# One attention kernel, three edits to its transfers: values stored in reading order, a head's large loads on ScalarE's queue, queries fetched four rows at a time

## The chip, the core and the metric

The kernel runs on one core of one Trainium2 chip. The metric is the device time of one execution in microseconds (us). Before the change, six runs gave a median of 5294.02 us (5281.08 to 5301.66).

## What is computed

The input is an image batch of 4 x 384 channels x 32 x 32. Two layers follow. Layer 0 is attention with relative positions, then a small feed-forward block. Layer 1 is a 7 x 7 depthwise convolution (several kernels folded into one), then a mixture of four experts. All of it is float32. Only the attention of layer 0 and the projections ahead of it are touched here:

```python
qkv = (xt @ w_qkv).reshape(b, n, 3, HEADS, hd).transpose(2, 0, 3, 1, 4)   # b=4, n=1024, 8 heads, hd=48
q, k, v = qkv[0] * scale, qkv[1], qkv[2]
attn = einsum('bhid,bhjd->bhij', q, k)
attn = attn + take_along_axis(einsum('bhid,hLd->bhiL', q, table_k), idx)          # 15 x 15 clipped offsets
attn = attn + take_along_axis(einsum('bhjd,hLd->bhjL', k * scale, table_q), idx).T
attn = softmax(attn)
out = einsum('bhij,bhjd->bhid', attn, v)
out = out + einsum('bhiL,hLd->bhid', wsum(attn, idx), table_v)
```

## The kernel before

There are three phases one after the other. The memory of one phase is given to the next, so the first instructions of a phase wait for the last transfers that read the memory of the one before.

**Projection (`qkv_phase`, 0 to 314 us).** Eight tiles of 512 tokens. Each is normalised over the channels and multiplied by the weights. Queries and keys go to a DRAM tensor `qk_d` (768 rows, one for each channel, 4096 tokens each). Values go to `v_d`, token by token: row = token, 384 channels, so that a head's part of a row is 192 bytes. The evacuations from PSUM alternate between ScalarE and VectorE. The stores are issued by GpSimd, one for `v_d` in each tile (768 KB).

**Attention (`attention_phase`, 314 to 2176 us).** The heads run one after the other. A head begins with `load_head`: the two offset tables into `tab`, the keys and the queries of all four images into `kq` (partitions 0 to 47 and 64 to 111), half of the keys again into `k2`. `prepare` multiplies tables with keys and queries: one result is transposed into `b2` in SBUF, the other goes through ScalarE copies (`st`, L218) to a DRAM scratch `sd`. Then `load_values` brings the head's values into `vb`, four DMAs of 192-byte runs; each value row is padded to 64 columns, and the padding is set to zero once.

The inner loop runs over the 32 rows `y` of the image. One step handles row `y` of all four images together (4 x 32 queries on 128 partitions). Its parts, with the lines that the profile names:

- `fetch(y + 2)`: one small DMA brings the queries of the row (`qs`, 24 KB), one brings its part of `sd` (`s1`, 240 KB, shown as `s`); GpSimd then adds the bias for the row (L249). `s1` has three buffers, so a fetch waits for an older row's bias.
- `scores`: PE multiplies queries with keys (`sc_ps`); VectorE adds the bias and takes the maximum in one instruction (L275).
- `exponentials`: ScalarE (L285).
- `far_sums` on VectorE (L296, L297), `transposes` on PE with copies by ScalarE (L305, L306), `windows` on PE and VectorE (L315, L320).
- after every four rows `values`: PE multiplies the weights with `vb` (`av_ps`), ScalarE copies the result (L338).
- after rows 15 and 31 `value_table`: the part of `table_v`, from the tile `tvw` (`tv_ps`, L367).

The tile `tvw` is loaded anew for each head in nine pieces, one in each of the rows 4 to 12: six of 384 KB with an outermost size of 4, then three of 192 KB. `normalise` (rows 2 and 18) loads the reciprocal sums into one buffer `rb`, half by half, and GpSimd multiplies (L379); `store` follows at rows 4 and 20. What is left of a head after its last row is done while the next head begins.

Order: every DMA of this phase is issued by SyncE, in the order in which the program calls `dma` (L146); PE, VectorE and ScalarE instructions are held in program order too (`pin`). SyncE can run ahead of the engines as far as its own waits allow, and an instruction that waits holds up all that is behind it on the same engine.

**Rest (`rest_phase`, 2176 to 5279 us).** Projection of the output, feed-forward, convolution and experts, one image after the other. The change doesn't touch it.

Of the kernel before, what the change touches and what calls it, by code (L numbers as in the profile page):

```python
# [10 lines left out]
F32 = mybir.dt.float32  # L11
# [6 lines left out]
P = 128  # L18
B, C, IMG = 4, 384, 32
N = IMG * IMG  # L20
NT = B * N
KC = C // P
HEADS, HD = 8, C // 8
# [4 lines left out]
NBLK = N // P  # L28
PADR = 6
AROWS = IMG + 2 * PADR  # L30
YB = 4
YT = 16
XT = 16
BIG = 3.0e38
FF = 1536
NF = FF // P
NEXP = 4
TOK = 512
# [38 lines left out]
def qkv_phase(tc, cst, x, w_qkv, qk_d, v_d):  # L77


    nc = tc.nc  # L80
    with ExitStack() as es:
        wp = es.enter_context(tc.tile_pool(name="q_w", bufs=1))
        work = es.enter_context(tc.tile_pool(name="q_work", bufs=2))
        ev = es.enter_context(tc.tile_pool(name="q_ev", bufs=4))
        psum = es.enter_context(tc.tile_pool(name="q_ps", bufs=2, space=PSUM))
        psmm = es.enter_context(tc.tile_pool(name="q_mm", bufs=4, space=PSUM))
        wq = wp.tile([P, KC, 3 * C], F32, name="wq")
        nc.sync.dma_start(wq, w_qkv.rearrange("(k p) n -> p k n", p=P))
        for t in range(NT // TOK):
            b, n0 = divmod(t * TOK, N)  # L90
            xt = work.tile([P, KC, TOK], F32, tag="xt", name="xt", bufs=3)
            nc.sync.dma_start(xt, x[b, :, n0 : n0 + TOK].rearrange("(k p) n -> p k n", p=P))
            xn = work.tile([P, KC, TOK], F32, tag="xn", name="xn")
            layer_norm(nc, (work, work, psum, "st"), cst["ones"], xt, xn, cst["eps6"])
            for m in range(2 * KC):
                ps = psmm.tile([P, TOK], F32, tag="mm", name="qk_ps")
                for k in range(KC):
                    nc.tensor.matmul(  # L98
                        ps, wq[:, k, m * P : (m + 1) * P], xn[:, k, :], start=(k == 0), stop=(k == KC - 1)
                    )  # L100
                sb = ev.tile([P, TOK], F32, tag="qk", name="qk_sb")
                if m % 2:
                    nc.vector.tensor_copy(sb, ps)
                else:
                    nc.scalar.copy(sb, ps)
                nc.gpsimd.dma_start(qk_d[m * P : (m + 1) * P, t * TOK : (t + 1) * TOK], sb)
            vs = ev.tile([P, TOK // P, C], F32, tag="v", name="v_sb", bufs=2)
            for j in range(TOK // P):
                ps = psmm.tile([P, TOK], F32, tag="mm", name="v_ps")
                for k in range(KC):  # L110
                    nc.tensor.matmul(
                        ps[:, :C], xn[:, k, j * P : (j + 1) * P], wq[:, k, 2 * C :], start=(k == 0), stop=(k == KC - 1)
                    )
                if j % 2:
                    nc.vector.tensor_copy(vs[:, j, :], ps[:, :C])
                else:
                    nc.scalar.copy(vs[:, j, :], ps[:, :C])
            nc.gpsimd.dma_start(v_d[t * TOK : (t + 1) * TOK, :].rearrange("(j p) c -> p j c", p=P), vs)


def attention_phase(tc, cst, tabs, tv, qk_d, v_d, ao_d, heads):
# [15 lines left out]
    nc = tc.nc  # L137

    def pin(ins):
        return tc.keep_in_program_order(ins)  # L140
# [3 lines left out]

    def dma(*args, **kw):
        pin(nc.sync.dma_start(*args, **kw))  # L146

    with ExitStack() as es:
        dram = es.enter_context(tc.tile_pool(name="a_dram", bufs=2, space=DRAM))
# [24 lines left out]
        kq = fixed.tile([64 + HD, NT], F32, name="kq")  # L174
        k2 = fixed.tile([64 + HD, B, N // 2], F32, name="k2")
        tab = fixed.tile([64 + HD, SPAN, ZW], F32, name="tab")
        vb = fixed.tile([P, B, NBLK, 64], F32, name="vb")
        nc.gpsimd.memset(vb, 0.0)
        b2 = fixed.tile([P, IMG, SPAN, IMG], F32, name="b2")
        b2f = b2.rearrange("p x e y -> p (x e y)")  # L180
        aT = fixed.tile([P, NBLK, YB, P], F32, name="aT")
# [4 lines left out]
            return bass.AP(ap.tensor, ap.offset + off, [list(ap.ap[0])] + dims)  # L186

        def load_head(h):
            dma(tab[0:HD], tabs[1, h])
            dma(tab[64 : 64 + HD], tabs[0, h])  # L190
            kd = qk_d[C + h * HD : C + (h + 1) * HD, :]
            dma(kq[0:HD, :], kd)
            dma(kq[64 : 64 + HD, :], qk_d[h * HD : (h + 1) * HD, :])
            dma(k2[64 : 64 + HD], kd.rearrange("p (b n) -> p b n", b=B)[:, :, N // 2 :])

        def load_values(h):
            for b in range(B):
                dma(
                    vb[:, b, :, :HD],
                    v_d[b * N : (b + 1) * N, h * HD : (h + 1) * HD].rearrange("(c p) d -> p c d", p=P),  # L200
                )

        def prepare(h):

# [19 lines left out]
                )  # L224
            return sd

        def fetch(s):

            h, y = s["h"], s["y"]
            s["qs"] = small.tile([HD, B, IMG], F32, tag="qs", name="qs")  # L230
            dma(
                s["qs"],
                qk_d[h * HD : (h + 1) * HD, :].rearrange("p (b n) -> p b n", b=B)[:, :, y * IMG : (y + 1) * IMG],
            )
            s1 = work.tile([P, SPAN, IMG], F32, tag="s1", name="s1", bufs=3)
            sd = s["sd"]
            dma(
                s1.rearrange("p e x -> p (e x)"),
                bass.AP(
                    sd.tensor, sd.offset + y * IMG * SPAN * IMG,  # L240
                    [[IMG * IMG * SPAN * IMG, B], [SPAN * IMG, IMG], [1, SPAN * IMG]],
                ),
            )
            bias = work.tile([P, IMG, IMG], F32, tag="bias", name="bias", bufs=3)
            c0, c1 = max(0, y - 6), min(IMG, y + 7)
            for y0, y1, e, step in ((c0, c1, c0 - y + 7, 1), (0, c0, 0, 0), (c1, IMG, SPAN - 1, 0)):
                if y0 < y1:
                    n = y1 - y0
                    nc.gpsimd.tensor_tensor(  # L249
                        bias[:, y0:y1, :],  # L250
                        shifted(b2f, e * IMG + y0, [[step * IMG + 1, n], [SPAN * IMG, IMG]]),
                        s1[:, e : e + n, :] if step else bcast(s1[:, e : e + 1, :], 1, n),
                        ALU.add,
                    )
            s["bias"] = bias
# [135 lines left out]
        def load_value_table(h):  # L391

            base = tv.offset + h * SPAN * ZW * HD
            for c in range(3):
                for i in range(0, IMG, IMG // 2):
                    dma(
                        tvw[:, c, i : i + IMG // 2].rearrange("p i d -> p (i d)"),
                        bass.AP(
                            tv.tensor, base + ((1 + 4 * c) * ZW + i) * HD,
                            [[ZW * HD, 4], [HD, IMG], [1, IMG // 2 * HD]],  # L400
                        ),
                    )
                    yield
            for i, e in enumerate((SPAN - 2, 0, SPAN - 1)):
                dma(
                    tvw[i * IMG : (i + 1) * IMG, 3].rearrange("p i d -> p (i d)"),
                    bass.AP(tv.tensor, base + e * ZW * HD, [[HD, IMG], [1, IMG * HD]]),
                )
                yield

        late = None
        for h in heads:
            load_head(h)
            sd = prepare(h)
            done = None
            if late is not None:
# [9 lines left out]
            for y in range(IMG):  # L426
                s = blk[y]
                if y + 2 < IMG:
                    fetch(blk[y + 2])
                if y >= 4:  # L430
                    next(pieces, None)
                if done and y % YT == 2:
                    normalise(done[1], done[2])
                if done and y % YT == 4:
                    store(done[0], done[1], done[3])
                    done = None
                if y + 1 < IMG:
                    scores(blk[y + 1])
                far_sums(s)
                bound = y % YB == 0  # L440
                if bound and y + 1 < IMG:
                    exponentials(blk[y + 1])
                if bound and y:
                    windows(blk[y - 1])
                    values(o, y - 1)
                    if y % YT == 0:
                        done = (h, o, value_table(h, o, y - 1), y - 1)
                if y % YT == 0:
                    o = work.tile([P, B // 2, YT * IMG], F32, tag="o", name="oT")
                transposes(s)  # L450
                if not bound:
                    windows(blk[y - 1])
                    if y + 1 < IMG:
                        exponentials(blk[y + 1])
# [254 lines left out]
def metaformer_kernel(ctx: ExitStack, tc: tile.TileContext, ins, out):  # L709
# [10 lines left out]
        nc.vector.memset(t, v)  # L720
        cst[name] = t
    qk_d = dram.tile([2 * C, NT], F32, name="qk_d")
    v_d = dram.tile([NT, C], F32, name="v_d")
    ao_d = dram.tile([C, NT], F32, name="ao_d")
    qkv_phase(tc, cst, ins["x"], ins["w_qkv"], qk_d, v_d)
    attention_phase(tc, cst, ins["tabs"], ins["tv"], qk_d, v_d, ao_d, list(range(HEADS)))
# [64 lines left out]
```

## Time and profile before

| | |
|---|---|
| median of six runs | 5294.02 us (5281.08 to 5301.66) |
| profiled execution | 5281.08 us, span of its instructions 5279.2 us |
| PE, VectorE, ScalarE, GpSimd busy | 82%, 46%, 23%, 19% of the span |
| granted TensorE clock, mean | 0.89 |
| phases | 0 to 314, 314 to 2176, 2176 to 5279 us |
| DMA engines busy in the three phases | 24%, 36%, 17% |
| PE busy in attention | 1422 of 1862 us |

The chain that ended last is followed back from the end of the program: at each step to what released the instruction. An entry "DMA s<-sd" there is the time from the issue of that transfer to its landing. In lists of instructions the numbers in front are the start and the duration in us; the brackets give the idle time of the engine just before, and what ended it; "SPq" is SyncE's issue of a DMA. "L285" is line 285 of the kernel.

### The profile page before, as it was taken

How to read it: one execution, taken by the hardware profiler on the slowest of the kernel's cores; microseconds unless marked ns; L12 is line 12 of the kernel's file. 1: busy time of each engine (PE TensorE's matmuls, PEld its weight loads, DVE VectorE, ACT ScalarE, POOL GpSimd, SP SyncE). 2: the span in 40 equal slices, each digit the busy share in tenths (PEclk: the TensorE clock that was granted, in tenths of full speed). 3: DMA queues.
4: the chain of work that ended last, by engine and by line, in shares of the span. 5: the costliest groups of instructions: out<-in, count | busy, mean ns of one | idle time of the engine just before them, and what ended most of it. 6: DMA issues, size and time to landing. Idle time of an engine off the chain costs nothing.

```text
span 5279.2 us, 55887 instructions
## 1 busy us (share of the span) xinstructions
PE 4349.0 (82%) x22816; PEld 2231.4 (42%) x22816; DVE 2444.9 (46%) x3220; ACT 1237.5 (23%) x2011; POOL 992.4 (19%) x798
## 2 busy tenths in 40 slices
PE   7867777877878777660789998799998899999999
PEld 3335555545555555320234343243442343444443
DVE  2237575766657576349288111494112781111111
ACT  1124443434434343210111111111112111111111
POOL 1226344353543535100000000100000000000000
PEclk9989898988889898875789899799998898989999
DMA  2242433424343342300012122022121121212211
GB/s 103 74 133 78 141 88 116 124 85 129 81 136 105 93 123 87 99 24 0 12 36 72 60 72 72 12 72 78 54 72 36 31 77 60 72 60 72 78 60 36
DMA packets 256880, 397.31 MB, mean 75 GB/s; under 512 B 100520, under 2 KB 182732, under 8 KB 255856
## 3 DMA queue, kind: packets, MB, share of 16 engines
q1 hardware_dynamic: 249584, 368.57, 23.0%
q0 software_dynamic: 7040, 25.17, 1.2%
q8 instruction: 180, 2.95, 0.2%
q14 instruction: 76, 0.62, 0.0%
HBM read 299.05 MB, written 94.63 MB: 75 GB/s over the span
## 4 chain that ended last, share of the span: by engine, by line
PE 65%; DVE 14%; DMA 8%; issue 7%; POOL 3%; ACT 3%; SPq 1%; POOLq 0%; DVEq 0%; ACTq 0%
PE y_ps L684 17%; PE e_ps L675 16%; DVE xb L642 5%; PE av_ps L143 4%; PE tabq_ps L143 3%; PE qk_ps L98 3%; DVE extra L297 3%; DMA s<-sd 2%; DMA qs<-qk_d 2%; PE sc_ps L143 2%; PE tv_ps L143 2%; PE t_ps L305 2%; PE ln_var L60 2%; DVE ln_rstd L64 2%; DMA kq<-qk_d 2%
## 5 line engine op out<-in xcount | busy, mean ns | idle before, releaser
L684 PE MATMUL y_ps<-hs,wb 128*128 128x512 f32 x2304 | 1080.4, 608 | 1.5 <-DVE hs L681 1.5
L675 PE MATMUL e_ps<-xn_e,wa 128*128 128x512 f32 x2304 | 1060.0, 600 | 0.0
L249 POOL TENSOR_TENSOR bias<-b,s 128x416 f32<-128x416 f32 (+24 forms) x656 | 791.3, 1241 | 919.3 <-DMA s<-sd 449.0
L681 DVE TENSOR_TENSOR hs<-hs,ge 128x512 f32<-128x512 f32 x384 | 263.9, 689 | 1310.7 <-ACT hs L680 1301.1
L642 DVE SCALAR_TENSOR_TENSOR xb<-img,w,xb 128x1024 f32<-128x1024 f32 x588 | 723.8, 1291 | 8.8 <-POOL img L67 8.8
L675 PEld LDWEIGHTS e_ps<-xn_e,wa 128*128 128x128 f32 x2304 | 443.4, 193 | 555.6 <-issue 555.5
L684 PEld LDWEIGHTS y_ps<-hs,wb 128*128 128x128 f32 x2304 | 417.4, 192 | 616.7 <-issue 402.6
L680 ACT ACTIVATE hs<-e_ps,c_b 128x512 f32<-128x512 f32 x384 | 263.8, 687 | 1733.7 <-PE e_ps L675 1694.6
L275 DVE CUSTOM_DVE_ANT_0 arow<-sc_ps,bias 128x1024 f32<-128x1024 f32 x256 | 311.7, 1218 | 372.2 <-POOL bias L249 277.1
L285 ACT ACTIVATE arow<-arow,nm 128x1024 f32<-128x1024 f32 x256 | 295.0, 1152 | 550.8 <-DVE nm L275 549.6
L689 POOL DMA_DIRECT2D out<-ot x8 | 6.5, 808 | 2177.5 <-DVE ot L688 2177.5
L305 PE MATMUL t_ps<-ident,arow 128*128 128x128 f32 x2048 | 311.0, 300 | 125.6 <-ACT arow L285 108.3
L143 PE MATMUL sc_ps<-kq,qs 48*32 48x512 f32 x2048 | 315.7, 682 | 102.8 <-DMA qs<-qk_d 102.8
L305 PEld LDWEIGHTS t_ps<-ident,arow 128*128 128x128 f32 x2048 | 245.1, 152 | 328.4 <-ACT arow L285 240.2
L296 DVE TENSOR_REDUCE extra<-arow 128x32 f32<-128x32 f32 (+24 forms) x512 | 354.4, 734 | 0.0
L306 ACT COPY aT<-t_ps 128x512 f32<-128x512 f32 x512 | 277.9, 588 | 294.5 <-PE t_ps L305 293.8
L60 PE MATMUL ln_var<-ln_sq,ones 128*128 128x512 f32 x192 | 127.6, 817 | 249.8 <-ACT ln_sq L57 249.8
L143 PE MATMUL sc_ps<-k,kq 48*32 48x512 f32 x2048 | 315.7, 682 | 0.0
L143 PE MATMUL av_ps<-aT,vb 128*64 128x128 f32 x4096 | 279.4, 303 | 0.0
L143 PEld LDWEIGHTS av_ps<-aT,vb 128*64 128x64 f32 x4096 | 263.9, 156 | 12.0 <-issue 7.6
L143 PE MATMUL tabq_ps<-tab,kq 48*128 48x480 f32 x512 | 229.6, 607 | 22.0 <-DMA kq<-qk_d 21.2
L143 PE MATMUL tabk_ps<-tab,kq 48*128 48x480 f32 x512 | 235.0, 615 | 15.2 <-DMA kq<-qk_d 15.2
(112 smaller groups left out, 3722.5 us busy)
## 6 DMA issues: line engine op xcount, KB each, us to landing
wa<-in_w SPq DMA_DIRECT2D x64, 1152.0 KB
wb<-in_w SPq DMA_DIRECT2D x64, 1152.0 KB
sd<-st SPq DMA_DIRECT2D x128, 480.0 KB
s<-sd SPq DMA_DIRECT2D x256, 240.0 KB
tvw<-in_tv SPq DMA_DIRECT2D x48, 384.0 KB
xt<-in_x SPq DMA_DIRECT2D x16, 768.0 KB
qk_d<-qk_sb POOLq DMA_DIRECT2D x48, 256.0 KB, 2.3
kq<-qk_d SPq DMA_DIRECT2D x16, 768.0 KB
```

Source lines behind the costliest of these rows:

```text
L143: pin(nc.tensor.matmul(*args, **kw))
L249: nc.gpsimd.tensor_tensor(bias[:, y0:y1, :], shifted(b2f, e * IMG + y0, [[step * IMG + 1, n], [SPAN * IMG, IMG]]), s1[:, e : e + n, :] if ...
L275: nc.vector.tensor_tensor_reduce(s["flat"], ps.rearrange("p h n -> p (h n)"), s["bias"].rearrange("p y x -> p (y x)"), -SCALE, BIG, ALU.ad ...
L285: nc.scalar.activation(s["flat"], s["flat"], AF.Exp, bias=s["nm"], scale=-1.0, accum_out=dn[:, y % YT : y % YT + 1])
L296: pin(nc.vector.tensor_reduce(ex[:, i, :], a[:, p0:p1, :].rearrange("p y x -> p x y"), AX.X, ALU.add))
L305: pin(nc.tensor.transpose(pt[:, j, :], s["flat"][:, k0 : k0 + P], ident))
L306: pin(nc.scalar.copy(aT[:, 4 * g : 4 * g + 4, s["y"] % YB, :], pt))
L642: nc.vector.scalar_tensor_tensor(acc[:, k], img[:, k, dy : dy + IMG, dx : dx + IMG], w7[:, k, dy, dx : dx + 1], acc[:, k], ALU.mult, ALU.add,)
L675: nc.tensor.matmul(ph, wa[:, k, f * P : (f + 1) * P], xn[:, k, :], start=(k == 0), stop=(k == KC - 1))
L680: nc.scalar.activation(hs, ph, AF.Gelu, bias=b1[:, e, ff : ff + 1])
L681: nc.vector.tensor_tensor(hs, hs, ge[:, e, :], ALU.mult)
L684: nc.tensor.matmul(py[m], wb[:, f, m * P : (m + 1) * P], hs, start=False, stop=last)
```

## The change

1. `v_d` becomes `[heads, 128, 4 images x 8 blocks x 64]`: for each head and partition, one run of 8 KB in the order in which `vb` is read. `qkv_phase` collects the values of all tokens in an SBUF tile `va` (64 KB a partition, set to zero once on GpSimd, so that the padding is stored too) and stores it after each image (2 MB) instead of after each tile. `load_values` is one DMA instead of four, and the memset of `vb` goes.
2. A second helper `bulk` issues DMAs on ScalarE's queue, pinned in program order there. `load_head`, `load_values` and the nine pieces of `tvw` use it. `load_head` of the next head is called in row 31, ahead of that row's `far_sums`; only the first head is loaded before the loop.
3. `qs` holds four rows (96 KB) and is fetched when `y` is a multiple of 4, into two buffers.

```diff
+        va = wp.tile([P, HEADS, B * NBLK, VW], F32, name="va")
+        nc.gpsimd.memset(va, 0.0)
...
+                dst = va[:, :, t * (TOK // P) + j, :HD]
+                src = ps[:, :C].rearrange("p (h d) -> p h d", d=HD)
                 if j % 2:
-                    nc.vector.tensor_copy(vs[:, j, :], ps[:, :C])
+                    nc.vector.tensor_copy(dst, src)
                 else:
-                    nc.scalar.copy(vs[:, j, :], ps[:, :C])
-            nc.gpsimd.dma_start(v_d[t * TOK : (t + 1) * TOK, :].rearrange("(j p) c -> p j c", p=P), vs)
+                    nc.scalar.copy(dst, src)
+            if n0 + TOK == N:
+                w = NBLK * VW
+                nc.gpsimd.dma_start(
+                    v_d.rearrange("h p n -> p h n")[:, :, b * w : (b + 1) * w],
+                    va[:, :, b * NBLK : (b + 1) * NBLK, :].rearrange("p h c d -> p h (c d)"),
+                )
...
+    def bulk(*args, **kw):
+        pin(nc.scalar.dma_start(*args, **kw))
...
-        nc.gpsimd.memset(vb, 0.0)
...
         def load_head(h):
-            dma(tab[0:HD], tabs[1, h])
-            dma(tab[64 : 64 + HD], tabs[0, h])
+            bulk(tab[0:HD], tabs[1, h])
+            bulk(tab[64 : 64 + HD], tabs[0, h])
...
-            dma(kq[0:HD, :], kd)
-            dma(kq[64 : 64 + HD, :], qk_d[h * HD : (h + 1) * HD, :])
-            dma(k2[64 : 64 + HD], kd.rearrange("p (b n) -> p b n", b=B)[:, :, N // 2 :])
+            bulk(kq[0:HD, :], kd)
+            bulk(kq[64 : 64 + HD, :], qk_d[h * HD : (h + 1) * HD, :])
+            bulk(k2[64 : 64 + HD], kd.rearrange("p (b n) -> p b n", b=B)[:, :, N // 2 :])
...
         def load_values(h):
-            for b in range(B):
-                dma(
-                    vb[:, b, :, :HD],
-                    v_d[b * N : (b + 1) * N, h * HD : (h + 1) * HD].rearrange("(c p) d -> p c d", p=P),
-                )
+            bulk(vb.rearrange("p b c d -> p (b c d)"), v_d[h])
...
-            s["qs"] = small.tile([HD, B, IMG], F32, tag="qs", name="qs")
-            dma(
-                s["qs"],
-                qk_d[h * HD : (h + 1) * HD, :].rearrange("p (b n) -> p b n", b=B)[:, :, y * IMG : (y + 1) * IMG],
-            )
+            if y % YB == 0:
+                qs[0] = small.tile([HD, B, YB * IMG], F32, tag="qs", name="qs", bufs=2)
+                dma(
+                    qs[0],
+                    qk_d[h * HD : (h + 1) * HD, :].rearrange("p (b n) -> p b n", b=B)[
+                        :, :, y * IMG : (y + YB) * IMG
+                    ],
+                )
+            s["qs"] = qs[0][:, :, y % YB * IMG : (y % YB + 1) * IMG]
...
-                    dma(
+                    bulk(
                         tvw[:, c, i : i + IMG // 2].rearrange("p i d -> p (i d)"),
...
-        for h in heads:
-            load_head(h)
+        load_head(heads[0])
+        for n, h in enumerate(heads):
             sd = prepare(h)
...
                 if y + 1 < IMG:
                     scores(blk[y + 1])
+                elif n + 1 < len(heads):
+                    load_head(heads[n + 1])
                 far_sums(s)
```

More of the change, by code (lines that the diff above doesn't have):

```diff
@@ L33 @@
 XT = 16
+VW = 64
 BIG = 3.0e38
@@ L106, in qkv_phase @@
                 nc.gpsimd.dma_start(qk_d[m * P : (m + 1) * P, t * TOK : (t + 1) * TOK], sb)
-            vs = ev.tile([P, TOK // P, C], F32, tag="v", name="v_sb", bufs=2)
             for j in range(TOK // P):
@@ L176, in attention_phase @@
         tab = fixed.tile([64 + HD, SPAN, ZW], F32, name="tab")
-        vb = fixed.tile([P, B, NBLK, 64], F32, name="vb")
-        nc.gpsimd.memset(vb, 0.0)
+        vb = fixed.tile([P, B, NBLK, VW], F32, name="vb")
         b2 = fixed.tile([P, IMG, SPAN, IMG], F32, name="b2")
@@ L225, in prepare @@
             return sd
+        qs = [None]
         def fetch(s):
             h, y = s["h"], s["y"]
-            s["qs"] = small.tile([HD, B, IMG], F32, tag="qs", name="qs")
-            dma(
-                s["qs"],
-                qk_d[h * HD : (h + 1) * HD, :].rearrange("p (b n) -> p b n", b=B)[:, :, y * IMG : (y + 1) * IMG],
-            )
+            if y % YB == 0:
[7 more added lines that the diff above has]
+            s["qs"] = qs[0][:, :, y % YB * IMG : (y % YB + 1) * IMG]
             s1 = work.tile([P, SPAN, IMG], F32, tag="s1", name="s1", bufs=3)
@@ L404, in load_value_table @@
             for i, e in enumerate((SPAN - 2, 0, SPAN - 1)):
-                dma(
+                bulk(
                     tvw[i * IMG : (i + 1) * IMG, 3].rearrange("p i d -> p (i d)"),
@@ L722, in metaformer_kernel @@
     qk_d = dram.tile([2 * C, NT], F32, name="qk_d")
-    v_d = dram.tile([NT, C], F32, name="v_d")
+    v_d = dram.tile([HEADS, P, B * NBLK * VW], F32, name="v_d")
     ao_d = dram.tile([C, NT], F32, name="ao_d")
```

## The prediction

> **What bounds the kernel now.** I read the page's chain first, because its by-line list says which transfers are ever the last thing waited for. Then I read the chain of waits of one head in order of time, and then the queues that feed it.
>
> ```profile
> PE 65%; DVE 14%; DMA 8%; issue 7%; POOL 3%; ACT 3%; SPq 1%; POOLq 0%; DVEq 0%; ACTq 0%
> ```
>
> The program is bound by compute; transfers are 8% of the chain. The by-line list behind it gives 2% each to kq, qs and s, some 105 us each, all in attention (314 to 2176 us, eight heads). No other part of the chain has to do with the edit. The chain of waits around the third head:
>
> ```profile
> 761.23 13.05 DMA kq<-qk_d
> ...
> 850.39 12.88 DMA qs<-qk_d
> ...
> 872.78 13.26 DMA s<-sd
> ```
>
> So a head pays 13 us at its boundary, and some 26 us of chain lie in transfers of rows 5 to 12. SyncE's own queue shows what they stand behind:
>
> ```profile
> 760.82 0.77 SPq L146 DMA_DIRECT2D kq<-qk_d  x2
> ...
> 810.04 7.78 SPq L146 DMA_DIRECT2D vb<-v_d  x4
> ...
> 859.65 0.77 SPq L146 DMA_DIRECT2D s<-sd  x1
> 860.47 3.05 SPq L146 DMA_DIRECT2D tvw<-in_tv  x1
> 863.62 2.69 SPq L146 DMA_DIRECT2D qs<-qk_d  x1
> 866.40 0.83 SPq L146 DMA_DIRECT2D s<-sd  x1
> ```
>
> The four vb loads hold the queue 7.8 us at the head's start. Later each row sends one s, one tvw piece and one qs, and s goes out every 6.5 us (859.65, 866.40), because the queue backs up: issues of 0.6 us elsewhere take 2.7 to 3.1 us here. The row times on ScalarE (start of each exponential) say what this costs:
>
> ```profile
> 836.68 1.15 ACT L285 ACTIVATE arow<-arow,nm 128x1024 f32<-128x1024 f32 x1 [1.19 <-DVE nm L275]
> 846.81 1.15 ACT L285 ACTIVATE arow<-arow,nm 128x1024 f32<-128x1024 f32 x1 [8.89 <-DVE nm L275]
> ...
> 863.44 1.15 ACT L285 ACTIVATE arow<-arow,nm 128x1024 f32<-128x1024 f32 x1 [3.31 <-DVE nm L275]
> 870.17 1.15 ACT L285 ACTIVATE arow<-arow,nm 128x1024 f32<-128x1024 f32 x1 [5.48 <-DVE nm L275]
> ```
>
> Rows 4, 5, 8 and 9 start at these times; from 4 to 5 it is 10.1 us. Rows 7 to 12 (857.02 to 890.92) take 6.8 us each; rows 19 to 31 (932.77 to 990.62), where the chain holds no transfer, take 4.8. Last, the rate in that stretch:
>
> ```profile
> 853.00:877.00 24.00, 17.40 (x187) 11.49 (x176) 11.03 (x22) 8.80 (x16) 12.14 (x12) 0.86 0.28 104
> ```
>
> The last two columns are DMA share and GB/s. A row's s, tvw piece and qs are 240 + 384 + 24 KB; at 104 GB/s that is 6.4 us, the row's pace. Rows wait for transfers while the DMA engines are 28% busy: the limit is a few engines or the order on the queue. That is the question the change turns on.
>
> [...]
>
> **The change, part by part.** Sums are against the profiled run, 5281.08 us (span 5279.2 and 1.9 around it); the median of the six is 12.9 above it, added at the end.
>
> *v_d and its writer.* The va memset is 16384 elements a partition; vb's of 2048 took 1.80 us, so some 14 us on GpSimd, which is idle until 27.50: nothing. The copies keep their number and size (0.48 and 0.56 us). The last store becomes 2 MB instead of 768 KB. The chain runs over its landing (309.35, 3.98 us) before the attention pools may start. 256 KB land in 2.3 us and 768 KB in 4.0, so 2 MB in about 8.2: +4 us, once. The removed vb memset (318.20) lies beside the kq load: 0.
>
> *Head loads to ScalarE, at row 31.* "One row early" is not early. SyncE already runs ahead: it issued kq at 760.82, when the last scores had read the old kq, and both tabs at 741.62. On ScalarE the five issues stand after the exponential of row 31 (763.03, 1.15 and 0.19 us, so 764.2) and kq stands behind two tabs (1.09 us for the two on SyncE): kq goes out at 765.3, 4.5 later. The tabs' 354 KB now run just ahead of it; head 0 had that order already and its wait was 13.93 against 13.05, so +0.9. The copies of row 31 behind these issues slip by 2 us, while PE waits for kq anyway (until 774.42). Sum 5.4 us at each of 7 boundaries, +38. Ends: 3.5, if ScalarE's queue issues while the exponential still runs, and 7, if the tabs cost their full share of the kq rate (354/1536 of 10 us).
>
> *Values.* The four loads become one with 8 KB a partition, issued after prepare's last copy (about 805.5), so the queue time of 7.8 us leaves SyncE. The s of row 2 then goes out at 810.6 instead of 818.65, and its bias can follow that of row 1 (ends 820.85) at once instead of at 824.59: 3.7 us earlier. What is late next is rb: GpSimd multiplies the first half (833.61) after the bias of row 4, SyncE holds the second rb and the s of row 5 behind that. All of this moves up by the same 3.7, and 0.6 more for the qs that no longer stands before s. Row 5 at 842.5 instead of 846.81: 4.3 us.
>
> *tvw to ScalarE.* Nine issues a head, between one exponential and the next copy. Bytes and shapes stay. Lower end of the gain: if the transfers of both queues simply share what one had, the stretch still ends when 8 s and 6 tvw pieces are through, and it keeps only its earlier start, 4.3, or up to 6.6 where s no longer stands behind a whole piece. Upper end: s passes tvw and rows 7 to 12 go at 4.8 instead of 6.8, 5 rows by 2.0, so 10 more, 14.3 in all. The nearest row for sharing is not in attention: the output stores (768 KB, GpSimd's queue) land in 7.1 us when expert weights are queued ahead of them, and in 4.0 at the end, when nothing is. A second queue did not pass the first there. So I stay near the lower end, 5 us a head for heads 1 to 7. Head 0 has no rb and sent its first tvw piece early (383.17), which ScalarE's order delays: 2. Sum -37.
>
> [...]
>
> *ScalarE's issues.* tvw and vb are ten issues of some 0.55 us. Six meet rows that wait for transfers (ScalarE idle 3.3 us before row 8's exponential); three or four meet rows at full pace, partly in the idle 0.8 us before a copy. 0.6 us a head, +5; ends 0 and 20.
>
> *qs by four rows.* 64 issues for 256, on SyncE, which is then no bound; waits of PE on qs are in the stretch above. Nothing more.
>
> Sum: +4 + 38 - 37 + 5 = +10, so 5291 in the profiled run and 5304 on the median's scale. I put 5302, as the first terms lean low.
>
> **The rivals.** *Shared transfers* (forecast, 50%): boundary and gain cancel. Own range 5284 to 5324.
>
> *s passes tvw* (30%). 14.3 us in seven heads and 4 in head 0 are 104; against +4, +38 and +12 of ScalarE's issues, now on rows at full pace, that is -50: 5244. For it: engines 28% busy, and s is never behind a whole piece. Against it: the output store's 7.1 us.
>
> *ScalarE's queue backs up* (20%, slower). Where tvw backs up, SyncE's issue takes 2.7 to 3.1 us instead of 0.5 to 0.6, and then it is ScalarE that stands, with exponential and copies behind it and PE's transposes behind those. 2.3 us for six pieces in eight heads is 110; rows that wait anyway hide about half: 5302 + 55 = 5357. It decides from an issue of about 2.2 us on: ScalarE's idle time before an exponential in this stretch is 3.3, and a row's copies take 1.1. Against it: ScalarE's queue holds one piece a row, where SyncE's held three transfers.
>
> *The head loads do not come earlier*, against what the edit's place suggests, is part of the forecast: were a boundary only as long as before, the sum would be 38 lower, 5264.
>
> **How the numbers follow.** About 0.2%, 10.6 us, is what a measurement of this kernel can tell from no change: 5283 to 5305. The forecast's 50% lie 5 below, 20 within, 25 above it; the second case is faster with 29 of 30; the third is slower. Faster 0.34, same 0.21, slower 0.45. The range 5238 to 5354 takes in the second case from a little below its price, and half of the third.
>
> **What would show it.** Right: kq issued by ScalarE some 4.5 us after the last scores, first matmul of the next head some 19 us after them (13.6 before); the s of row 2 out within 1 us of row 1's; row 5 some 4 us earlier after row 0; rows 7 to 12 still above 6 us; ScalarE's tvw issues at 0.6 us. Rows 7 to 12 near 5 us mean the second case; tvw issues over 2 us on ScalarE, with idle PE behind the copies, the third. A boundary no longer than before would break my largest term.

## The result, and the profile after

The changed kernel takes 5306.1 us in the median of 23 runs (5294.05 to 5333.08), the kernel before 5292.7 us in 47 (5270.87 to 5308.44). The ratio is 1.0033, with a 95% interval of 1.0024 to 1.0043: slower by 13 to 23 us. The two profiled executions lie further apart, 5314.87 and 5281.08 us, since the one of after is above its median and the one of before below: the stages below account for the 34 us between these two executions, and the medians for about half of that.

All of it is in attention. The page's chain of after, by engine and by line:

```profile
PE 60%; DVE 13%; DMA 11%; issue 7%; POOL 5%; ACT 2%; SPq 1%; ACTq 0%; POOLq 0%; DVEq 0%
PE y_ps L700 17%; PE e_ps L691 16%; DMA s<-sd 7%; DVE xb L658 5%; POOL bias L263 3%; PE tabq_ps L153 3%; PE qk_ps L102 3%; PE av_ps L153 2%; DVE extra L311 2%; PE ln_var L61 2%; DVE ln_rstd L65 2%; DMA kq<-qk_d 2%; PE o_ps L635 2%; PE f_ps L632 2%; PE tv_ps L153 1%
```

Transfers have 11% of the chain instead of 8%. qs is no longer among the lines listed, and s has 7% where it had 2%. (Line numbers moved: L299 is the exponential that was L285, L320 the copy that was L306; L156 is SyncE's helper, L159 ScalarE's.) The chain of waits of the fourth head, in order of time (start, duration, what):

```profile
1002.70 13.85 DMA kq<-qk_d
...
1047.03 8.09 DMA sd<-st
...
1056.33 8.50 DMA s<-sd
...
1093.29 17.30 DMA s<-sd
...
1117.00 14.93 DMA s<-sd
```

In the chain of the third head before, shown with the prediction, kq had 13.05, no store of `sd` was among the long pieces, and two pieces of 13 us stood in the rows. ScalarE's list shows where its own issues stand (idle time in brackets):

```profile
1001.38 1.15 ACT L299 ACTIVATE arow<-arow,nm 128x1024 f32<-128x1024 f32 x1
1001.39 0.79 ACTq L159 DMA_DIRECT2D tab<-in_tabs  x2
1002.22 0.43 ACTq L159 DMA_DIRECT2D kq<-qk_d  x1
...
1110.60 0.54 ACTq L159 DMA_DIRECT2D tvw<-in_tv  x1
1111.24 1.07 ACT L320 COPY aT<-t_ps 128x512 f32<-128x512 f32 x2 [13.51 <-DMA s<-sd]
```

The exponential of row 31 and the first tab issue start together, here and at the six other boundaries (0.01 us apart): ScalarE sent the tab while the exponential, 1.15 us long, still ran. The last two lines are new: a copy on ScalarE came 13.5 us late because a tvw issue ahead of it waited for an s to land, a transfer of SyncE's with which it shares no data. In the list of ScalarE's waits (total us, times, longest) this is

```profile
ACT aT L320 <- DMA s<-sd: 130.4, 13, 13.6
```

and the list of before has no such line. The semaphores in the instruction records say why. In this kernel eight of them serve all loads and stores of SyncE and ScalarE (736 and 120 issues), mostly in turn: of the 691 issues between 318 and 2210 us, 486 have the semaphore of the issue eight before, and 504 wait until an earlier transfer with their own semaphore has landed, whichever of the two engines sent that one. The piece issued at 1110.60 has the semaphore of the s that SyncE sent at 1093.29 and that took 17.30 us.

The stages, in us, from the starts of the exponentials (rows) and of the first tabq matmul; "row 31 to tabq" and "tabq to row 0" are means over the seven boundaries, the rows means over the eight heads:

| kernel | first row 0 at | row 31 to tabq | tabq to row 0 | rows 0-5 | 5-13 | 13-31 |
|---|---|---|---|---|---|---|
| before | 371.2 | 11.4 | 44.6 | 26.5 | 47.4 | 98.5 |
| after | 378.5 | 15.6 | 48.0 | 23.4 | 47.6 | 98.1 |
| a1_tvw_sync | 378.1 | 15.4 | 47.0 | 23.0 | 45.3 | 98.8 |
| a2_head_sync | 377.8 | 11.4 | 46.2 | 23.0 | 47.3 | 98.4 |
| a3_vb_row1 | 373.2 | 15.8 | 44.2 | 22.5 | 46.5 | 97.7 |
| a4_tvw16 | 378.9 | 15.4 | 46.9 | 24.0 | 33.8 | 97.0 |
| b1_values_only | 375.7 | 11.4 | 44.4 | 25.8 | 47.3 | 100.4 |
| b2_queries_only | 370.9 | 11.5 | 43.8 | 26.0 | 47.3 | 99.6 |
| b3_tvw16_on_before | 369.8 | 11.2 | 43.6 | 28.7 | 33.0 | 99.3 |
| b4_best_guess | 375.5 | 11.1 | 44.3 | 27.2 | 31.9 | 97.4 |
| c5_all_sync | 375.5 | 11.5 | 44.2 | 29.5 | 32.8 | 98.7 |
| c6_s_in_four | 373.5 | 11.5 | 44.0 | 21.3 | 36.5 | 93.1 |
| d1_queries_tvw16 | 372.7 | 11.3 | 44.7 | 28.1 | 32.3 | 98.7 |
| e1_in_four_scalar | 374.0 | 11.5 | 44.3 | 21.9 | 34.1 | 95.8 |

Before to after: +7.3 at the start, seven times (4.2 + 3.4), eight times -3.3 in the rows: 7.3 + 53 - 26 = 34.

### The profile page after: what moved, and what is told of

It reads as the page before. It is cut to its first block, busy times and chain, and to the rows that moved or that the text cites. A ratio compares the mean times of both kernels' runs of the same rounds, so it can differ in the third digit from the quotient of the medians.

```text
span 5313.1 us, 55461 instructions
## 1 busy us (share of the span) xinstructions
PE 4325.8 (81%) x22816; PEld 2218.1 (42%) x22816; DVE 2467.7 (46%) x3220; ACT 1233.6 (23%) x2011; POOL 1001.8 (19%) x794
## 4 chain that ended last, share of the span: by engine, by line
PE 60%; DVE 13%; DMA 11%; issue 7%; POOL 5%; ACT 2%; SPq 1%; ACTq 0%; POOLq 0%; DVEq 0%
PE y_ps L700 17%; PE e_ps L691 16%; DMA s<-sd 7%; DVE xb L658 5%; POOL bias L263 3%; PE tabq_ps L153 3%; PE qk_ps L102 3%; PE av_ps L153 2%; DVE extra L311 2%; PE ln_var L61 2%; DVE ln_rstd L65 2%; DMA kq<-qk_d 2%; PE o_ps L635 2%; PE f_ps L632 2%; PE tv_ps L153 1%
## 5 line engine op out<-in xcount | busy, mean ns | idle before, releaser
L299 ACT ACTIVATE arow<-arow,nm 128x1024 f32<-128x1024 f32 x256 | 295.6, 1155 | 432.1 <-DVE nm L289 395.6
L320 ACT COPY aT<-t_ps 128x512 f32<-128x512 f32 x512 | 276.2, 589 | 407.9 <-PE t_ps L319 269.0
L153 PE MATMUL sc_ps<-kq,qs 48*32 48x512 f32 x2048 | 303.1, 658 | 7.5 <-DMA qs<-qk_d 7.5
L153 PE MATMUL sc_ps<-k,kq 48*32 48x512 f32 x2048 | 303.0, 658 | 0.0
L329 PE MATMUL a_ps<-ident,arow 128*128 128x128 f32 x768 | 146.9, 305 | 141.8 <-DVE a1t L334 96.0
L153 PE MATMUL tabk_ps<-tab,kq 48*128 48x480 f32 x512 | 237.2, 620 | 28.7 <-DMA kq<-qk_d 28.7
```

Of the source, the lines that this page charges most:

```text
L153: pin(nc.tensor.matmul(*args, **kw))
L299: nc.scalar.activation(s["flat"], s["flat"], AF.Exp, bias=s["nm"], scale=-1.0, accum_out=dn[:, y % YT : y % YT + 1])
L320: pin(nc.scalar.copy(aT[:, 4 * g : 4 * g + 4, s["y"] % YB, :], pt))
```

## The experiments

Ratios are to the kernel before, on the same chip and in the same rounds. A difference to the changed kernel is worked out by dividing the ratio by 1.0033; it carries both uncertainties, some 10 us. The ratios of c5, c6 and d1 have wider intervals, and differences between them and the other versions are known to some 20 us. Each stage is read from one execution.

**a1_tvw_sync: the table's pieces back on SyncE.**

```diff
-                    bulk(
+                    dma(
                         tvw[:, c, i : i + IMG // 2].rearrange("p i d -> p (i d)"),
...
-                bulk(
+                dma(
                     tvw[i * IMG : (i + 1) * IMG, 3].rearrange("p i d -> p (i d)"),
```

> The changed kernel with the nine value-table pieces of a head back on SyncE's queue. In the changed kernel ScalarE stood 13.5 us ahead of a copy (1097.7 to 1111.2) because its tvw issue waited for a transfer of SyncE's, an s, to land. Theory 1, these waits of ScalarE hold up the rows: without them the rows gain 3 to 5 us a head, 25 to 40 us in all, some 5270 to 5280. Theory 2, the rows wait for the s transfers anyway and ScalarE's wait only stands beside that: within 10 us of the changed kernel, some 5296 to 5316, with rows 5 to 12 again at 6.5 us each.

1.0004 (0.9992 to 1.0016), some 15 us faster than the changed kernel: between the two theories. Rows 5 to 13 take 45.3 instead of 47.6. With the table on ScalarE's queue a head costs about 2 us more, 15 us in all, against 130 us of waits before the copies: so most of these seem to lie beside rows that wait for s anyway.

**a2_head_sync: `load_head` back on SyncE.**

```diff
         def load_head(h):
-            bulk(tab[0:HD], tabs[1, h])
+            dma(tab[0:HD], tabs[1, h])
...
-            bulk(kq[0:HD, :], kd)
+            dma(kq[0:HD, :], kd)
```

> The changed kernel with load_head back on SyncE's queue, called at the same place in row 31. Theory 1, kq went out 3 us later on ScalarE and behind the two tabs, and PE waits for it: the wait to the first tabq matmul shrinks by 3.9 us at each of seven boundaries, 27 us in all, some 5279. Theory 2, the rest of row 31 and the values matmuls on PE cover the later load: no change, 5306. ScalarE's five issues are gone in both.

0.9958 (0.9942 to 0.9974), some 40 us faster than the changed kernel. Theory 1 (27 us) holds and a little more: row 31 to tabq is 11.4 again, 4.2 shorter, and the stretch behind it 1.8 shorter. The chain of waits at one of its boundaries begins right behind the last scores:

```profile
984.88 1.13 PE sc_ps L153 x16
...
986.39 12.75 DMA kq<-qk_d
```

**a3_vb_row1: the values load out of the way of `sd`.**

```diff
-            load_values(h)
...
+                if y == 1:
+                    load_values(h)
```

> The changed kernel with the one values load issued in row 1 instead of straight after prepare. Theory 1, the 1 MB load ran into the last stores of sd, so that the last of these landed 8.1 us after its issue instead of 2.6 and the first s went out late: from the first table matmul to the first exponential of a head it should take 50 us again instead of 53 to 54, 3.5 us in eight heads, 28 in all, some 5278. Theory 2, this is hidden beside the value table's matmuls of the head before: no change, 5306.

0.9956 (0.9940 to 0.9973), some 41 us faster than the changed kernel. tabq to row 0 is 44.2 instead of 48.0, the first head starts 5 us earlier, and the last store of `sd` in its chain of waits lands in 2.6 us, where the changed kernel had 8.09 (over the eight heads 2.6 to 4.9 us here, 6.5 to 8.4 in the changed kernel, 2.6 to 4.5 before):

```profile
1040.80 2.60 DMA sd<-st
```

Theory 1 is shown. From the first table matmul to row 0 this run gains some 30 us in all, what was expected; the rest of the 41 lies in the rows.

**a4_tvw16: the table in pieces with an outermost size of 32.**

```diff
-            for c in range(3):
-                for i in range(0, IMG, IMG // 2):
+            for c in range(4):
+                for i in range(4 if c < 3 else 3):
+                    e = 1 + 4 * c + i if c < 3 else (SPAN - 2, 0, SPAN - 1)[i]
                     bulk(
-                        tvw[:, c, i : i + IMG // 2].rearrange("p i d -> p (i d)"),
-                        bass.AP(
-                            tv.tensor, base + ((1 + 4 * c) * ZW + i) * HD,
-                            [[ZW * HD, 4], [HD, IMG], [1, IMG // 2 * HD]],
-                        ),
+                        tvw[i * IMG : (i + 1) * IMG, c].rearrange("p i d -> p (i d)"),
+                        bass.AP(tv.tensor, base + e * ZW * HD, [[HD, IMG], [1, IMG * HD]]),
                     )
...
-                if y >= 4:
+                if y >= 1:
                     next(pieces, None)
```

> The changed kernel with the value table loaded in 15 pieces of 192 KB with an outermost size of 32, rows 1 to 15, instead of six of 384 KB with an outermost size of 4 and three of 192 KB; same bytes, still on ScalarE's queue. Theory 1, the pieces with an outermost size of 4 use few of the DMA engines, the same ones as s, and this sets the pace of rows 5 to 12: rows go at 4.8 us, 8 to 13 us a head gained, 65 to 100 us in all, some 5206 to 5241, and ScalarE no longer waits over 10 us for an s. Theory 2, the pace comes from the order of the queues or the rate at which these tables can be read: within 15 us of the changed kernel, or slower by six more issues a head on ScalarE, 0.5 us each, 5306 to 5330.

0.9809 (0.9794 to 0.9825), some 118 us faster than the changed kernel. Rows 5 to 13 take 33.8 instead of 47.6, 13.8 us in each head: theory 1, above its upper end.

**b1_values_only: the kernel before with the values part alone, on SyncE.** The edit is part 1 of the change, with one line different (the source line is shortened here):

```diff
         def load_values(h):
-            for b in range(B):
-                dma(vb[:, b, :, :HD], v_d[b * N : ...])
+            dma(vb.rearrange("p b c d -> p (b c d)"), v_d[h])
```

> The kernel before with the values part of the change alone: va, the 2 MB stores, one 1 MB load of values, issued by SyncE at the old place (after the fetches of rows 0 and 1). Theory 1, as the prediction had it: the 7.8 us in which the four loads held SyncE's queue are gone, the s of row 2 goes out at once, row 5 comes 3 to 4 us earlier in each head, 4 us are lost once at the start: 20 to 28 us faster than before, some 5269. Theory 2, the load still stands ahead of the s of row 2 with as many bytes, and takes the DMA engines for some 4 us there: 0 to 10 us, some 5290. In neither does it run into the stores of sd, since SyncE sends it after the first two s, which wait for those.

0.9990 (0.9975 to 1.0004): theory 2. Rows 0 to 5 take 25.8 instead of 26.5, and the start is 4.5 us later. So the long runs are not what gains the 3.1 us that the changed kernel has in rows 0 to 5. That leaves the load's leaving SyncE's queue, by elimination: a1 and a2, which put the table and the head loads back there, keep 23.0, and b2 has 26.0.

**b2_queries_only: the kernel before with the queries part alone.**

> The kernel before with the queries part alone, four rows in one load. Theory 1, as the prediction had it: qs only waits in line behind others, so its 256 issues cost nothing of their own: within 8 us of before. Theory 2, a qs takes a place in the line of SyncE's eight transfers and 0.6 us of issue in each row while the queue is backed up, and PE waited 103 us for qs in all: 2 to 4 us a head, 16 to 32 us faster.

0.9967 (0.9955 to 0.9978), 12 to 24 us faster than before: theory 2 in size. Its stages differ from those of before by at most 1.1 us a head, and the profile of before is one of its faster executions, so these two traces don't show where the 17 us are. One figure goes with them: the granted clock is 0.889 to 0.892 in the five runs of b2 and 0.885 to 0.890 in the 17 of before. Among those 17, a clock higher by 0.001 goes with some 3.6 us less, so the difference of the means, 0.003, would be some 11 of the 17 us. Whether the edit raises the clock or these five runs happened to have it stays open.

**b3_tvw16_on_before: a4's edit, with `dma`, on the kernel before.**

> The kernel before with the value table loaded in 15 pieces of 192 KB with an outermost size of 32 in rows 1 to 15, on SyncE's queue. If the shape of the six pieces sets the pace of rows 5 to 12 whichever queue they stand in: 8 to 13 us a head as in a4_tvw16 on the changed kernel, 65 to 105 us faster than before, some 5190 to 5230. If a4's gain came from ScalarE no longer standing for long at its tvw issues, there is none to be had here: within 15 us of before.

0.9757 (0.9738 to 0.9777), some 129 us faster than before, above the range of theory 1. Rows 5 to 13 fall from 47.4 to 33.0 with no ScalarE queue in play, so the cause lies in how the table is cut, in whichever queue it stands. The two traces differ by 100 us: rows 5 to 13 gain 115, rows 0 to 5 lose 18. The edit changes more than the outermost size: pieces of half the bytes, runs of 6 KB instead of 3, and rows 1 to 15 instead of 4 to 12. Row starts 8 to 10 on ScalarE, and the window in which rows 7 to 10 run (last two columns DMA share and GB/s):

```profile
836.04 1.15 ACT L285 ACTIVATE arow<-arow,nm 128x1024 f32<-128x1024 f32 x1 [0.86 <-DVE nm L275]
839.60 1.15 ACT L285 ACTIVATE arow<-arow,nm 128x1024 f32<-128x1024 f32 x1 [2.32 <-DVE nm L275]
847.57 1.16 ACT L285 ACTIVATE arow<-arow,nm 128x1024 f32<-128x1024 f32 x1
```

```profile
826.00:850.00 24.00, 20.18 (x211) 13.22 (x210) 18.38 (x31) 12.22 (x22) 20.49 (x20) 0.86 0.44 124
```

The share went from 0.28 to 0.44 and the rate from 104 to 124 GB/s. GpSimd is now busy 20.49 of the 24 us, where it had 12.14; its bias may be what limits these rows next, which no run tests.

The packet records of the traces say what the pieces shared. In the window of before that the prediction shows (853 to 877), exactly four packets of s and of the 384 KB pieces were in flight for 79% of the time in which any were. A 3 KB packet took 0.123 us, so four at a time are an estimated 100 GB/s, and the window had 104. During the kq load of the same trace (761 to 774) it was 16 packets of kq for 70% of the time. In the changed kernel, with s on SyncE's queue and the table on ScalarE's (1080 to 1130), it is again four for 79%, with a share of 0.32 and 110 GB/s: neither the second queue nor the other order brought more of them. Which of the 16 engines carried a packet the records don't say.

**b4_best_guess: a2, a3 and a4 together.**

> The changed kernel with load_head on SyncE, the values load in row 1 and the value table in 15 pieces (a2, a3 and a4 together). If the three are at different places of a head, they add up: a4 measured 5191, and a2 and a3 gained some 33 us each against the changed kernel, so some 5125 to 5140. If the boundary wait and the late s of row 0 cover each other in part, 5140 to 5165. Not below 5100.

0.9747 (0.9733 to 0.9760), 5160: the three don't add up, as the second expectation had it. Row 31 to tabq and rows 5 to 13 do as expected. From tabq to row 0 it gains 2.6 over a4, where a2 and a3 gained 1.8 and 3.8; and rows 0 to 5 take 27.2 where a4 had 24.0. ScalarE's list of the fourth head shows waits there:

```profile
1017.04 0.32 ACTq L159 DMA_DIRECT2D tvw<-in_tv  x1
1017.40 1.07 ACT L320 COPY aT<-t_ps 128x512 f32<-128x512 f32 x2 [8.10 <-DMA rb<-rd]
...
1024.54 0.32 ACTq L159 DMA_DIRECT2D tvw<-in_tv  x1
1024.89 0.59 ACT L320 COPY aT<-t_ps 128x512 f32<-128x512 f32 x1 [5.28 <-DMA ao_d<-oT]
```

Two table issues wait for transfers of SyncE's, and copies behind them with them. That these waits make rows 0 to 5 longer is not shown: c5 below has none of them and takes 29.5, and e1, which is b4 with s in four loads, takes 21.9.

**c5_all_sync: b4 with every `bulk` turned into `dma`.**

> b4_best_guess with every load of attention on SyncE, so that ScalarE issues no DMA. In b4 a row's copies stood 8.1 and 5.3 us behind tvw issues that waited for SyncE's transfers to land, rb among them. Theory 1, ScalarE's queue costs more than it gives, because an issue there waits for the transfer eight before it in the program's order, wherever that was issued: without it rows 1 to 4 lose these waits, 5 to 13 us a head, 40 to 100 us in all against b4 (5160), some 5060 to 5120. Theory 2, moving loads off SyncE does free its queue: SyncE then holds up the s of the rows as before, and the time is 5160 or more.

0.9801 (0.9767 to 0.9835), 5190: some 28 us slower than b4, with intervals that just don't meet, and theory 1 falls. ScalarE's waits are gone, but SyncE's queue is held longer. In its list the four rb loads hold it for 17.55 us (14.12 before, from 821.86 in the third head), the s of a later row behind them:

```profile
1017.41 17.55 SPq L156 DMA_DIRECT2D rb<-rd  x4
1035.00 0.56 SPq L156 DMA_DIRECT2D s<-sd  x1
```

Rows 0 to 5 take 29.5. While s is one load, ScalarE's queue both costs (the waits of 8.10 and 5.28 us in b4) and gives (some 28 us against c5).

**c6_s_in_four: c5 with each s in four loads.**

```diff
-            dma(
-                s1.rearrange("p e x -> p (e x)"),
-                bass.AP(
-                    sd.tensor, sd.offset + y * IMG * SPAN * IMG,
-                    [[IMG * IMG * SPAN * IMG, B], [SPAN * IMG, IMG], [1, SPAN * IMG]],
-                ),
-            )
+            for b in range(B):
+                dma(
+                    s1[b * IMG : (b + 1) * IMG].rearrange("p e x -> p (e x)"),
+                    bass.AP(
+                        sd.tensor, sd.offset + (b * IMG + y) * IMG * SPAN * IMG,
+                        [[SPAN * IMG, IMG], [1, SPAN * IMG]],
+                    ),
+                )
```

> c5_all_sync with each row's s (240 KB, outermost size 4) loaded as four transfers of 60 KB with an outermost size of 32. Theory 1, the shape with an outermost size of 4 holds a transfer to a few engines: s lands in some 3 us instead of 5, the head's first exponential comes 2 to 3 us sooner, 15 to 40 us faster than c5. Theory 2, transfers are no longer what rows wait for once the value table is in 15 pieces: no change, or slower by the three more issues of 0.5 us in each row and by taking four of the eight places in line, up to 60 us slower.

0.9670 (0.9638 to 0.9702), 5117, some 70 us faster than c5 and beyond theory 1's range: with e1 the fastest version. Bytes, runs (1920 bytes) and queue are as in c5; each s is now four transfers. From 1000 to 1060 us packets of s are in flight eight or more at a time for 49% of the time in which any are; in c5 there are never that many, and exactly four for 54%. Rows 0 to 5 take 21.3 instead of 29.5 and rows 13 to 31 93.1 instead of 98.7, while rows 5 to 13 lose 3.7. That may be the four s and a piece of the table in each row on one queue: e1, with the table on ScalarE's, takes 34.1 there instead of 36.5. The expected place was wrong: the first exponential came 2 us sooner in head 0 (1.1 of it before its first table matmul) and 0.2 in the others. Transfers are 3% of its chain:

```profile
PE 67%; DVE 16%; issue 7%; ACT 3%; DMA 3%; POOL 3%; SPq 1%; POOLq 0%; DVEq 0%; ACTq 0%
```

**d1_queries_tvw16: before with the queries part and the table in 15 pieces.**

> The kernel before with the queries part and the value table in 15 pieces, all on SyncE, the values as before in four loads of 192-byte runs. If the values part is worth something once the table no longer sets the pace: slower than c5 by 15 to 40 us (the four loads hold SyncE 7.8 us in each head, of which row 2 gave back 3.7). If not: within 10 us of c5. b3 had 5173, and the queries part alone 17 us on the kernel before, so 5155 to 5170 here.

0.9790 (0.9757 to 0.9822), 5179, above the 5155 to 5170 expected: some 6 us from c5 by the ratios, so the values part shows no worth on SyncE's queue once the table is out of the way either. The queries part shows no gain here over b3 (0.9757, 0.9738 to 0.9777), unlike in b2; the intervals meet.

**e1_in_four_scalar: c6 with values and table on ScalarE's queue.**

> c6_s_in_four with the values load and the value table's pieces issued by ScalarE, as in b4_best_guess; so b4 with s in four. It asks again what ScalarE's queue is worth, now where transfers are short. Theory 1, what b4 was better than c5 by (0.5%, 30 us) comes from SyncE having fewer issues in rows 1 to 15: it holds here, and more so, since SyncE now issues four s a row: some 5075 to 5095. Theory 2, with four s a row the line of eight reaches back two rows only, and ScalarE's issues wait for young transfers: as c6 or slower, 5115 to 5150.

0.9676 (0.9655 to 0.9696), 5121, as c6: theory 2. With s in four loads it makes no measurable difference which of the two queues carries values and table. Against b4, whose edit is the same but for s, it is some 38 us faster, so the gain of c6 comes again with the table on the other queue.

## Why the prediction was right or wrong

The forecast, 5302 in a range of 5238 to 5354, holds, and so does its story that the boundaries eat what the rows gain, since the transfers on two queues together got hardly more than one queue had (110 GB/s from 1080 to 1130, 104 from 853 to 877 before). But its terms were less right than their sum, and that the medians came within 4 us of it (5306) is in part luck: between the two traces the sum was +34 where I had +10.

- *First store, +4.* Right: the first table matmul came at 327.5 instead of 323.4, and the store took 7.51 us to land (`309.44 7.51 DMA v_d<-va`) where I had 8.2.
- *Boundary, +5.4 seven times.* Mechanism right, shown by a2; the size was 4.2. I counted the exponential of row 31 ahead of the tab issues; they start with it, so kq went out 3.2 us later and not 4.5. That is the case behind the lower end that I had named, 3.5. The wait behind tabs was sized rightly: from kq's issue to the first tabq matmul it is 14.6 us instead of 13.6, and I had 0.9 more.
- *Values load, no cost.* This step failed. "Issued after prepare's last copy" names its place exactly, and I counted there what the move takes from SyncE's queue, not what the 1 MB runs into: the last stores of `sd`, for which the first s waits. It cost 3.4 us in seven boundaries and about 3 in the first head, some 27 us; a3 shows it.
- *Row 5 earlier by 4.3.* 3.1, part of what was expected; row 2 came 4.6 us after row 1 instead of 6.6, as hoped, but row 3 took 6.8 instead of 3.8. Its bias stood on GpSimd behind the first multiplication by rb, and that waited for rb to land; head 0, which has no rb, took 4.9. I had that multiplication behind the bias of row 4. GpSimd's list of the fourth head:

```profile
1073.81 1.27 POOL L393 TENSOR_TENSOR oT<-oT,rb 128x512 f32<-128x512 f32 x1 [3.81 <-DMA rb<-rd]
1075.03 5.98 POOL L263 TENSOR_TENSOR bias<-b,s 128x320 f32<-128x320 f32 x4
```

- *Rows 7 to 12 stay near the lower end.* Right in sum: rows 5 to 13 take 47.6 against 47.4. They look different: rows at 3 us, then stalls of 9 to 16. That the second queue does not pass the first I had taken from the output store; here four packets at a time were in flight for 79% of the time, on two queues as on one.
- *ScalarE's issues, +5.* The issue itself was sized rightly (median 537 ns, 0.55 assumed). What the step left out is the wait ahead of it: 130 us of ScalarE in 13 places. The table's place on ScalarE's queue is worth some 15 us by a1, issues and waits together.
- *The rival "ScalarE's queue backs up"* had the right victim and the wrong cause: no issue of the table there took over 1.9 us, but the wait for a shared semaphore, 13.6 us at the longest, did what a full queue was to do.
- *The rival "s passes tvw".* It did not. Its price for rows at full pace was low rather than high: a4 and b3 gained 14 us a head in rows 5 to 13, where I had 10.
- *Queries, nothing.* b2 says 17 us on the kernel before, in a place that its trace doesn't show; d1 says nothing over b3.

So +34 was made of 29 (boundaries), 31 (start and values load) and -26 (rows), where I had 38, 4, -37 and 5. Errors of 9 us at the boundaries and 6 in the rows in what I had counted, which nearly cancel, and one of 27 in what I hadn't.

On the question that the prediction left open, a few engines or the order on the queue, the runs speak against the order: the same bytes on the same queue, cut so that the outermost size is 32, were worth 2.4% (b3) and 1.3% (c6), and the other order on two queues in the changed kernel left the packets in flight at four. That it was a few engines is not shown. It is my estimate from the four packets at a time and the share of 0.28 where they held (four of 16 would be 0.25), against 0.44 in b3. A second issuing engine made no measurable difference between c6 and e1 (0.9670 and 0.9676); what made b4 faster than c5 (0.9747 and 0.9801) is open, since no run parts issue time from waits there.

## What to carry to other kernels

When rows wait for transfers and the DMA engines are far from busy (28% here), look at the outermost size of the access patterns before moving transfers to another queue: the same bytes in a shape with 32 outermost instead of 4 gained 2.4% here; the moves between queues gave from 0.3% slower (the table, a1) to 0.5% faster (values and table, b4 against c5). Before you move a transfer, ask what is in flight at its new place and who waits for that, not only what it frees at the old one. Ask the same of the waits of an issue on a compute engine's queue: those of the table on ScalarE's, for shared semaphores, held up copies for 130 us in 13 places.

## What the runs showed that I had not expected

- ScalarE sent a DMA while its exponential ran: they started at 1001.38 and 1001.39, and the exponential took 1.15 us.
- With an outermost size of 4, loads on two queues together had four packets in flight for 79% of the time, as on one queue.
- One load of 1 MB (values) beside the last stores of 480 KB stretched the landing of the last of these from 2.6 to 8.1 us in the fourth head.
- Of two queues, neither was the better place once s came in four loads (0.9670 and 0.9676); and where it didn't, b4 was faster than c5 in spite of ScalarE's visible waits of 8.1 and 5.3 us.
